# First attention of a two-layer sequence kernel: keys and receptances by seven block products

## The chip, the cores and the metric

The kernel runs on one core of one Trainium2 chip. The metric is the device time of one execution in microseconds (us). The core has engines that run side by side, each with its own queue in a fixed order: TensorE (PE in the profile; PEld are its weight loads) multiplies matrices into PSUM, VectorE (DVE) and ScalarE (ACT) work element by element and can read PSUM, GpSimd (POOL) works on SBUF alone, and SyncE (SP) issues most of the DMAs. An engine waits for another through semaphores, and an instruction that waits holds up all that stand behind it in its queue.

## The reference

Two layers, each an attention and a feed-forward part with a layer norm behind each. The change lies in the first attention, over 16 sequences of 256 tokens and 256 channels, with 16 heads of 128:

```python
xx = jnp.concatenate([jnp.zeros_like(hidden_states[:, :1]), hidden_states[:, :-1]], axis=1)
xk = hidden_states * time_mix_k + xx * (1.0 - time_mix_k)
xv = hidden_states * time_mix_v + xx * (1.0 - time_mix_v)
xr = hidden_states * time_mix_r + xx * (1.0 - time_mix_r)
receptance = jax.nn.sigmoid(jnp.einsum('bth,oh->bto', xr, Wr))
key = jnp.einsum('bth,oh->bto', xk, Wk)
value = jnp.einsum('bth,oh->bto', xv, Wv)
...
def step(state, inp):
    rt, kvt = inp                      # kvt = key * value
    out = (state + u * kvt) * rt       # u = time_first
    new_state = state * w + kvt        # w = exp(-exp(time_decay))
    return (new_state, out)
...
return jnp.einsum('bto,ho->bth', attn, Wo)
...
x = _layernorm(x + attention)
```

The first feed-forward part (gate, up and down products with dequantized integer weights) follows, then the second layer with another attention and a mixture of experts.

## The kernel before

The 4096 tokens are cut into 8 blocks of 512 (two sequences each). The first attention loops over blocks and, in each, over the 16 heads. Everything is float32, so that every matmul of the program appears as two instructions in the profile. The 256 input channels are two chunks of 128 rows, so each projection is two accumulating matmuls.

- `load_xT` (L296) brings the block's transposed input; `mixed` (L339) makes the three mixtures: a scaled copy `mt` on ScalarE (L346) and a multiply-add `xm` on VectorE (L349), two of each for a mixture. The next block's mixtures are traced in the middle of a block.
- `head` (L374) is one head: `project` (L360; matmul L363) for keys, receptances and values, each into a PSUM bank of 128x512 `proj`; ScalarE copies the keys to SBUF (`k_sb`, L380) and takes the sigmoid of the receptances (`r_sb`, L382); VectorE multiplies keys and values (`kv`, L384), scans along each of the two sequences (`st`, L389) and adds the first term (`su`, L398); GpSimd multiplies by the receptances (`wkv`, L407).
- `out_project` (L410; matmul L412) adds the head's output, four tiles of 128 tokens, into four PSUM tiles `o_ps` that gather all 16 heads. It runs two heads behind.
- `added` (L185) adds a finished block to `x` (L189) and normalizes it on VectorE (`moments`, L150 and L151; `rsqrt`, L141 and, on GpSimd, L142; `normalize`, L166).
- All weights of this stage are loaded at the start (L329, L333) and stay. `dequantized` (L255) turns the feed-forward's integer weights into float32 (L271 on VectorE); its loads are issued from ScalarE's queue, in block 0 behind head 12. The fills of two DRAM buffers (`res_d`, `xp_d`) are issued from SP, one DMA a block in blocks 1 to 5, each behind a sigmoid.

The order of the engines' queues in this stage is made by the framework's scheduler; `manual_schedule` blocks, in which the queues of the listed engines keep the order in which the program is traced, stand in later stages only.

## Time and profile before

| what | us |
|---|---|
| median of 4 runs | 2216.14 (2213.14 to 2216.55) |
| the profiled execution, its own time | 2211.11 |
| its span in the profile | 2209.3 |
| first matmul of the stage starts | 6.78 |
| last output matmuls of the stage (L412) start | 891.58 |
| first matmul of the feed-forward part (L208) starts | 894.61 |

A row of a group of instructions reads: line, engine, operation, output and inputs, shapes, count | busy time in us, mean ns of one | idle time of the engine just before them, and what ended most of it. A row of the timeline reads: start in us, duration in us (of the whole merged group), engine, line, operation, names, shapes, count, and in brackets the engine's idle time before it and what ended it. A row of the view of waits reads: who waited, for whom, us in total, times, longest. A matmul's duration in the rows contains its way through the array; the distance between the starts of two is what it costs in a full stream.

### The profile page before, as it was taken

To read this page: it belongs to the slowest core of one execution; us is meant where nothing else is said; L and a number is where in the kernel's file an instruction comes from. 1 tells how busy PE (TensorE), PEld (TensorE's weight loads), DVE (VectorE), ACT (ScalarE), POOL (GpSimd) and SP (SyncE) were. 2 spreads that over 40 slices of the span, in tenths; PEclk is the share of its full clock that TensorE was granted. 3 is DMA by queue.
4 is the path that set the end of the run, shared out by engine and by line. 5 is a ranking of instruction groups with operands and counts; after the bars stand their busy time and mean duration, and the time that the engine had idled before them with its cause. 6 is when DMAs were issued, how large, how long until landed. Compare 5 with 4: busy or idle time off the path is not lost. (4 is left out here: it accounts for less than half of the span.)

```text
span 2209.3 us, 26585 instructions
## 1 busy us (share of the span) xinstructions
PE 2106.3 (95%) x8776; PEld 1301.9 (59%) x8776; DVE 1258.2 (57%) x3468; ACT 779.6 (35%) x2205; POOL 831.3 (38%) x972
## 2 busy tenths in 40 slices
PE   8999999999999999999998999999999999979878
PEld 4555555555555555555564666666666666656656
DVE  4464535353535343232326669798887979863435
ACT  3121212121212111211314665656566565521323
POOL 3121212121212121000004555657576766733556
PEclk9999999999999999999998999999999999999989
DMA  9120202020300000300000000000000000041347
GB/s 288 45 97 1 86 1 86 0 86 0 102 1 0 0 1 1 89 15 19 1 0 1 1 1 1 23 8 6 3 4 2 3 3 2 10 180 51 102 144 275
DMA packets 78234, 96.13 MB, mean 44 GB/s; under 512 B 14495, under 2 KB 70023, under 8 KB 75920
## 3 DMA queue, kind: packets, MB, share of 16 engines
q1 hardware_dynamic: 62320, 81.95, 11.4%
q10 hardware_dynamic: 6560, 7.30, 1.0%
q0 software_dynamic: 9216, 5.19, 0.9%
q8 instruction: 69, 1.13, 0.2%
q14 instruction: 69, 0.57, 0.1%
HBM read 62.69 MB, written 49.61 MB: 51 GB/s over the span
## 5 line engine op out<-in xcount | busy, mean ns | idle before, releaser
L407 POOL TENSOR_TENSOR wkv<-su,r_sb 128x512 f32<-128x512 f32 x128 | 164.9, 1288 | 682.6 <-DVE su L398 646.8
L384 DVE TENSOR_TENSOR kv<-k_sb,proj 128x512 f32<-128x512 f32 x128 | 88.0, 687 | 412.7 <-PE proj L363 412.7
L971 POOL TENSOR_TENSOR pr<-pr,rr 128x256 f32<-128x256 f32 (+1 forms) x256 | 207.1, 836 | 158.7 <-DVE rr L969 111.7
L958 ACT ACTIVATE pr<-sm,nm 128x128 f32<-128x128 f32 (+1 forms) x512 | 226.5, 446 | 96.3 <-DVE nm L945 88.9
L380 ACT COPY k_sb<-proj 128x512 f32<-128x512 f32 x128 | 74.9, 585 | 522.3 <-PE proj L363 509.2
L363 PE MATMUL proj<-xm,w_Wk 128*128 128x512 f32 x512 | 242.5, 596 | 6.8 <-DVE xm L349 6.8
L412 PEld LDWEIGHTS o_ps<-w_o,wkv 128*128 128x128 f32 x1024 | 194.4, 190 | 90.9 <-issue 68.2
L412 PE MATMUL o_ps<-w_o,wkv 128*128 128x256 f32 x1024 | 245.2, 379 | 1.6 <-POOL xb L298 1.5
L363 PE MATMUL proj<-xm,w_Wv 128*128 128x512 f32 x512 | 240.7, 592 | 1.1 <-ACT r_sb L382 1.1
L363 PE MATMUL proj<-xm,w_Wr 128*128 128x512 f32 x512 | 240.8, 593 | 0.0
L934 PE MATMUL s_ps<-kT,qT 128*128 128x128 f32 (+1 forms) x1024 | 199.0, 338 | 25.1 <-DVE nm L945 20.8
L916 POOL TENSOR_TENSOR qT<-qT,turned 128x512 f32<-128x512 f32 x128 | 162.8, 1274 | 88.9 <-DVE turned L915 88.9
L934 PEld LDWEIGHTS s_ps<-kT,qT 128*128 128x128 f32 x1024 | 146.6, 194 | 46.4 <-issue 32.7
L988 ACT COPY aT<-a_ps 128x384 f32<-128x384 f32 x256 | 109.8, 481 | 171.9 <-PE a_ps L984 171.9
L363 PEld LDWEIGHTS proj<-xm,w_Wr 128*128 128x128 f32 x512 | 97.5, 190 | 119.6 <-issue 118.1
L363 PEld LDWEIGHTS proj<-xm,w_Wv 128*128 128x128 f32 x512 | 97.2, 190 | 117.6 <-issue 115.4
L389 DVE TENSOR_TENSOR_SCAN st<-decay,kv 128x255 f32<-128x255 f32 x256 | 164.2, 683 | 3.9
L945 DVE CUSTOM_DVE_ANT_0 sm<-s_ps,const 128x128 f32<-128x128 f32 (+1 forms) x512 | 154.1, 354 | 16.5 <-PE s_ps L934 13.5
L830 POOL DMA_INDIRECT xp_d<-xs,dest x128 | 132.2, 1033 | 57.1 <-issue 31.1
L363 PEld LDWEIGHTS proj<-xm,w_Wk 128*128 128x128 f32 x512 | 97.7, 191 | 77.3 <-issue 63.7
L142 POOL TENSOR_TENSOR rstd<-rs_t,nhalf 128x4 f32<-128x4 f32 (+1 forms) x33 | 33.1, 1004 | 273.4 <-DVE rs_t L141 272.7
L997 PE MATMUL c_ps<-aT,kf 128*64 128x256 f32 (+1 forms) x1024 | 111.5, 339 | 19.2 <-ACT aT L988 19.2
(176 smaller groups left out, 3278.4 us busy)
## 6 DMA issues: line engine op xcount, KB each, us to landing
res_d<-zeros SPq DMA_DIRECT2D x4, 4096.0 KB
res<-res_d SPq DMA_DIRECT2D x16, 1024.0 KB
w_e<-in_W_experts_dram SPq DMA_DIRECT2D x32, 384.0 KB
xp_d<-empty SPq DMA_DIRECT2D x1, 5440.0 KB
xe<-xp_d SPq DMA_DIRECT2D x32, 170.0 KB
xb<-in_xT_dram SPq DMA_DIRECT2D x16, 256.0 KB
xs<-in_x_dram SPq DMA_DIRECT2D x32, 128.0 KB
out_dram<-os ACTq DMA_DIRECT2D x7, 512.0 KB
```

What stands on the lines that cost most here:

```text
L363: nc.tensor.matmul(ps, lhsT=w3[name][:, c, h * P : (h + 1) * P], rhs=xm[:, c, :], start=(c == 0), stop=(c == DC - 1),)
L389: nc.vector.tensor_tensor_scan(st[:, s, 1:], decay[:, h : h + 1].to_broadcast([P, S - 1]), kv[:, s, : S - 1], 0.0, ALU.mult, ALU.add,)
L407: nc.gpsimd.tensor_tensor(wkv, su, r_sb, ALU.mult)
L412: nc.tensor.matmul(os[tt], lhsT=wkv[:, tt * P : (tt + 1) * P], rhs=w_o[:, h, :], start=(h == 0), stop=(h == NH - 1),)
L830: put = nc.gpsimd.indirect_dma_start(out=xp_d[:, :], out_offset=bass.IndirectOffsetOnAxis(ap=dest[:, k, t : t + 1], axis=0), in_=xs[b][:, ...
L916: nc.gpsimd.tensor_tensor(qT, qT, qr, ALU.add)
L934: nc.tensor.matmul(ps[:, lo:hi], lhsT=qT[:, s * S + i * P : s * S + (i + 1) * P], rhs=kT[:, s * S : s * S + hi - lo], start=True, stop=True,)
L945: nc.vector.tensor_tensor_reduce(out=sm[:, lo:hi], in0=self.ps[s][:, lo:hi], in1=cst["mask"][:, lo:hi], scale=-(DQ**-0.5), scalar=-MASKED, ...
L958: nc.scalar.activation(self.pr[:, s, lo:hi], self.sm[s][:, lo:hi], AF.Exp, bias=self.nm[:, s, i : i + 1], scale=-1.0, accum_out=self.rs[:, ...
L971: nc.gpsimd.tensor_tensor(self.pr[:, :, lo:hi], self.pr[:, :, lo:hi], rr[:, :, i : i + 1].to_broadcast([P, 2, hi - lo]), ALU.mult,)
L988: copy = nc.scalar.copy(aT, a_ps)
L997: mm = nc.tensor.matmul(c_ps[k * KVLR : (k + 1) * KVLR, s, i * P :], lhsT=kf[:, 2 * s + i, :KVLR], rhs=aT[:, : 2 * P] if i == 0 else aT[:, ...
```

## The change

Heads are taken in pairs. For one pair, the keys of two heads (2 x 128 outputs) over the block's two sequences (2 x 256 tokens) from two chunks of channels are a 2 x 2 by 2 x 2 block product, eight products of 128x128 weights with 256 columns of input. After the change they are seven products (the Winograd form of Strassen's method), of sums of weight blocks with sums of input blocks, each alone in half a PSUM bank, and the results are put together by additions on VectorE. The same goes for the receptances. The values keep their eight.

The parts:

- `seven` issues the seven matmuls into four PSUM tiles `one`, `two`, `five` and `end` (the pool's four banks), copies the first product to SBUF on ScalarE, and adds on VectorE: three additions of 128x512 and one of 128x256, each with one input in PSUM and each using the result of the one before.
- `weight_sums` makes the sums of weight blocks in block 0, by eight GpSimd operations of 128x128 a pair, and SP writes them to DRAM (`wsum_d`). From block 1 on `load_weights` reads them from there. Weights are no longer kept: three buffers each, loaded two pairs ahead by SP.
- `mixed` is a generator that makes one mixture at a time, with four subtractions of 128x256 for the keys' and the receptances': for block 0 on VectorE (keys) and GpSimd (receptances), for the later blocks on GpSimd. They are placed behind pairs 3, 4 and 5 of the block before.
- `Pair` holds the parts of `head`, the sigmoid now in place in SBUF. The stage runs inside `manual_schedule`: step m has the keys of pair m, then the second scan, `su`, wkv product and the output of the pair before, values, receptances and first scan of pair m.
- `out_project` gathers into two PSUM tiles of a whole bank. The first matmul into a bank in a block runs over 512 columns (the weights of head 0 and a block of zeros behind them) so that it clears the bank.
- `block_end` replaces `added`: the additions, the moments and the normalizing (now on ScalarE) are three pieces, placed in the following steps; those of the last block go into the feed-forward part, behind its first Silu.
- `dequantized` issues its loads from SP and is cut into ten pieces, one behind each pair of block 1 and the first two of block 2. Each fill becomes four DMAs, one behind every second pair.
- The states' zero columns and the exponentials of the decay are made once at the start.

The diff, cut to its core:

```diff
-        nc.scalar.dma_start(out=sc, in_=a[f"s_{name}"].partition_broadcast(P))
+        nc.sync.dma_start(out=sc, in_=a[f"s_{name}"].partition_broadcast(P))
...
-                nc.scalar.dma_start(out=q[at : at + n, :], in_=wq[c : c + n, :])
+                nc.sync.dma_start(out=q[at : at + n, :], in_=wq[c : c + n, :])
...
+            yield
+    A11, A12, S1, A22, S2, S3, S4 = range(7)
+    B11, B21, B22, T1, T2, T3, NT4 = range(7)
+    C11, C12, C21, C22 = range(4)
...
+        def weight_sums(w3, p, eng):
+            for i, n in enumerate(SUMS):
+                w = w3[n]
+                for to, x, y, op in (
+                    (S3, A11, S1, ALU.subtract),
+                    (S1, S1, A22, ALU.add),
+                    (S2, S1, A11, ALU.subtract),
+                    (S4, A12, S2, ALU.subtract),
+                ):
+                    eng.tensor_tensor(w[:, to, :], w[:, x, :], w[:, y, :], op)
                 nc.sync.dma_start(
...
+                    out=wsum_d[i * NPR + p], in_=w.rearrange("p k o -> p (k o)")
+                )
+
+        def mixed(xb, k_eng, r_eng):
+            for j, n in ((1, "Wv"), (0, "Wk"), (2, "Wr")):
+                xm = pm.tile([P, 4 if n == "Wv" else 7, S], F32, tag=f"xm{j}", name="xm")
...
+                if n != "Wv":
+                    eng = k_eng if n == "Wk" else r_eng
+                    for to, x, y in ((T3, B22, T1), (T1, T1, B11), (T2, B22, T1), (NT4, B21, T2)):
+                        eng.tensor_tensor(xm[:, to, :], xm[:, x, :], xm[:, y, :], ALU.subtract)
+                yield n, xm
+
+        def seven(w, x, dst):
+            one, two, five, end = [
+                ps_p.tile([P, 2, S], F32, tag="proj", name=f"{n}_ps") for n in ("p1", "p2", "p5", "p3")
+            ]
+            for to, at, bt in (
+                (one[:, 0], A11, B11),
+                (two[:, 0], A12, B21),
+                (two[:, 1], S2, T2),
+                (one[:, 1], S3, T3),
+                (five[:, 0], S1, T1),
+                (end[:, 0], S4, B22),
+                (end[:, 1], A22, NT4),
+            ):
+                nc.tensor.matmul(to, lhsT=w[:, at, :], rhs=x[:, bt, :], start=True, stop=True)
+            t = phd.tile([P, 1, S], F32, tag="t", name="t_sb")
+            nc.scalar.copy(t[:, 0], one[:, 0])
+            yield
+            add = nc.vector.tensor_tensor
+            add(dst[:, C11 : C12 + 1], t.to_broadcast([P, 2, S]), two, ALU.add)
+            add(dst[:, C21], dst[:, C12], one[:, 1], ALU.add)
+            add(dst[:, C12::2], dst[:, C12 : C21 + 1], five[:, 0:1].to_broadcast([P, 2, S]), ALU.add)
+            add(dst[:, C12 : C21 + 1], dst[:, C12 : C21 + 1], end, ALU.add)
+            yield
...
+        with tc.manual_schedule(engines=engines):
...
+            for m in range(NM + 1):
...
+                for e in ends:
+                    next(e)
+                if m == 0:
+                    new.values(0)
+                if new:
+                    keys = new.sums("Wk")
+                    next(keys)
+                if old:
+                    old.scan(1)
+                if new:
+                    if m == 0:
+                        xms.update(mixing)
+                    next(keys)
+                    if b == 0 and p + 1 < NPR:
+                        weight_sums(weights[0], p + 1, nc.gpsimd)
+                if old:
+                    old.add_first(1)
+                    old.times_r(1)
+                    old.out_project(0)
+                for e in ends:
+                    next(e)
+                if new:
+                    new.values(0 if m else 1)
+                    rec = new.sums("Wr")
+                    next(rec)
+                    new.scan(0)
+                    new.add_first(0)
+                    next(rec)
+                    sigmoid = new.sigmoid()
+                if old:
+                    old.out_project(1)
+                for e in ends:
+                    next(e)
+                ends = []
+                if old and old.p == NPR - 1:
+                    ends.append(block_end(old.b))
+                if new:
+                    if m:
+                        new.values(1)
+                    new.times_r(0)
+                    if p in (3, 4, 5) and b + 1 < NB:
+                        if p == 3:
+                            mixing, xms_next = mixed(xb, nc.gpsimd, nc.gpsimd), {}
+                        n, xm = next(mixing)
+                        xms_next[n] = xm
+                    if b in (1, 2):
+                        next(dequantizing, None)
+                    if p % 2 and 1 <= b <= K + 1:
+                        after(fill(b, p // 2), sigmoid, "in this block")
+                old = new
+        next(ends[0])
...
+                with tc.issue_after(last_of["ACT"]):
+                    for _ in ends[0]:
+                        pass
...
-        "Wr": v["L0_attn_Wr"].T,
-        "Wk": v["L0_attn_Wk"].T,
-        "Wv": v["L0_attn_Wv"].T,
+        "Wr": pairs(v["L0_attn_Wr"].T),
+        "Wk": pairs(v["L0_attn_Wk"].T),
+        "Wv": pairs(v["L0_attn_Wv"].T),
```

## The prediction

> **What bounds the kernel now.** I read the page's busy times first, then the stretch from 400 to 500 us, then the timeline of a few heads of the first attention. The page:
>
> ```profile
> PE 2106.3 (95%) x8776; PEld 1301.9 (59%) x8776; DVE 1258.2 (57%) x3468; ACT 779.6 (35%) x2205; POOL 831.3 (38%) x972
> ...
> L363 PE MATMUL proj<-xm,w_Wk 128*128 128x512 f32 x512 | 242.5, 596 | 6.8 <-DVE xm L349 6.8
> ```
>
> The stretch (PE, weight loads, DVE, ACT, POOL, clock, DMA share, GB/s) and the timeline, where a head's keys begin:
>
> ```profile
> 400.00:500.00 100.00, 100.00 (x291) 55.11 (x291) 49.10 (x82) 21.02 (x35) 21.03 (x32) 1.00 0.14 48
> ...
> 400.46 1.88 PE L363 MATMUL proj<-xm,w_Wk 128*128 128x512 f32 x4
> 405.61 1.89 PE L412 MATMUL o_ps<-w_o,wkv 128*128 128x256 f32 x8
> 405.88 0.69 DVE L384 TENSOR_TENSOR kv<-k_sb,proj 128x512 f32<-128x512 f32 x1 [4.03 <-PE proj L363]
> 406.61 1.27 DVE L389 TENSOR_TENSOR_SCAN st<-decay,kv 128x255 f32<-128x255 f32 x2
> 407.34 1.88 PE L363 MATMUL proj<-xm,w_Wk 128*128 128x512 f32 x4
> 407.98 0.75 DVE L398 SCALAR_TENSOR_TENSOR su<-kv,vecs,st 128x512 f32<-128x512 f32 x1
> ```
>
> TensorE never rests, at the full granted clock, and sets the end of this stage; VectorE is half busy. A head takes 407.34 - 400.46 = 6.88 us: 12 instructions of 512 columns at 0.43 (four keys in 402.18 - 400.46) and 8 of 256 at 0.215. So an instruction costs its columns, also at 256, where the loads (190 ns) just fit. A pair is 13.75 us, the stage 64 pairs.
>
> **The products.** Keys and receptances of a pair were 16 instructions of 512 columns (6.88 us); they become 2 x 7 products of 256 columns, two instructions each: 28 x 0.215 = 6.02. A pair falls to 12.89, and 64 x 0.86 = **-55.0 us**. Opening the paired output banks lets two matmuls of each block run over 512 columns instead of 256: 2 x 2 x 0.215 x 8 blocks = **+6.9**.
>
> **VectorE.** Each product set adds four VectorE additions, three of 512 columns and one of 256. The nearest rows have the same shapes, one input in PSUM and one in SBUF:
>
> ```profile
> L384 DVE TENSOR_TENSOR kv<-k_sb,proj 128x512 f32<-128x512 f32 x128 | 88.0, 687 | 412.7 <-PE proj L363 412.7
> L349 DVE SCALAR_TENSOR_TENSOR xm<-xb,rest,mt 128x512 f32<-128x512 f32 x48 | 38.9, 836 | 7.2 <-ACT mt L346 4.2 <-PE proj L363 2.6
> L189 DVE TENSOR_TENSOR xs<-o_ps,xs 128x256 f32<-128x256 f32 x32 | 13.0, 412 | 13.4 <-PE o_ps L412 13.4
> ```
>
> Each addition needs the one before it, so what counts is the step to a dependent instruction: 406.61 - 405.88 = 0.73, and 0.44 for 256 columns; four take 2.63. Bounds for a long one: 0.60 (an independent follower starts that soon in the trace, 130.82 to 131.42) and 0.84 (the xm row); I take 0.73, as kv is the same operation; at 0.60 the late steps below mostly vanish and the sum falls by 25, at 0.84 it rises by 44. Per pair VectorE has 2 x 2.63 of additions and 2 x (0.73 + 1.37 + 0.75) of kv, scans and su: 10.96, some 10.3 with independent ones overlapping, of 12.89.
>
> In a plain step, from its first key product: keys to 3.01, output of the older pair's first head to 4.73, values to 6.45, receptances to 9.46, output to 11.18, values to 12.89. VectorE: kv from 0.26 (0.26 after the values' last matmul, as at 405.88), scans to 2.6, key additions to 5.1, su to 5.8; kv at 6.7 when the values land, scans and su to 9.5, receptance additions to 12.1. Sigmoid and GpSimd's product follow to 14.3, 1.4 into the next step, where the output needs it at 3.0; the four product banks are free by 5.1 (wanted at 6.45) and 12.1 (wanted at 12.89). So a plain step stays with TensorE, and so does a block's end (four additions 1.7, statistics 2.4): **0**; without that spare 2 us each would cost its length.
>
> **Sharing between VectorE and GpSimd.** In the old order GpSimd's wkv falls into VectorE's rest. Where it did not:
>
> ```profile
> 223.21 1.27 POOL L407 TENSOR_TENSOR wkv<-su,r_sb 128x512 f32<-128x512 f32 x1 [5.57 <-DVE su L398]
> 223.59 2.10 DVE L349 SCALAR_TENSOR_TENSOR xm<-xb,rest,mt 128x512 f32<-128x512 f32 x2 [0.53 <-PE proj L363]
> ...
> 227.69 1.41 DVE L349 SCALAR_TENSOR_TENSOR xm<-xb,rest,mt 128x512 f32<-128x512 f32 x2
> ```
>
> The same pair takes 2.10 beside GpSimd and 1.41 without: it starts about 0.15 before GpSimd ends. kv, with an input in PSUM, is not held (0.68 at 125.98, beside a wkv), the scans are (1.62 for two at 126.69). So scans, su and mixing exclude GpSimd's products, one at a time.
>
> **Steps that mix the next block.** Three steps of blocks 0 to 6 end with two scaled copies on ScalarE and two VectorE mixes, traced behind the sigmoids; the second and third add four GpSimd subtractions. On VectorE: 2.0 idle after the last addition (0.15 to ScalarE, the two sigmoids 1.0, a copy 0.70, 0.15 back), mixes 1.36, kv and the wait for a subtraction 0.79, scans 1.27, additions 2.53, su 0.65, kv 0.73, a wait for the wkv product 0.61, scans 1.37, su 0.65, additions 2.63: 14.6, against 12.89. Queued behind the mixes is the kv that frees the keys' additions, and then TensorE waits for banks and for wkv. The first such step is absorbed by the spare 2 us; the next two lose 1.65 and 1.7, the recovery 1.2: 4.55 a block. Blocks 3 to 6: 18.2; block 2 with six small dequantizing pieces 5.3; block 1 with four of 1.03 us (0.82 and 0.21 at L271) 6.7: **+30.2**. A subtraction is 0.63 by the nearest row (128x256), bounds 0.63 and 1.04, the latter worth 13 in all:
>
> ```profile
> L971 POOL TENSOR_TENSOR pr<-pr,rr 128x512 f32<-128x512 f32 x128 | 133.5, 1043 | 0.0
> ...
> L971 POOL TENSOR_TENSOR pr<-pr,rr 128x256 f32<-128x256 f32 x128 | 80.4, 628 | 158.7 <-DVE rr L969 111.7 <-PE s_ps L934 16.5 <-DVE top L778 14.3
> ```
>
> **Weight sums.** In block 0 each step puts eight 128x128 operations on GpSimd ahead of the older pair's product. The line through the two rows gives 0.42 each (bounds 0.3 and 0.63), 3.4 a step: covered in plain steps. In the mixing steps subtractions (2.5), sums (3.4) and the waits between come before the product, which ends some 5 us late: **+6.5** for block 0, 5 to 13 at the bounds. From block 1 the sums come from DRAM: 18 blocks of 64 KB in 12.89 us, 92 GB/s of the 319 of the first 30 us, requested two steps (25.8 us) ahead on SP. Ahead of them there can stand a fill waiting for the sigmoid, up to 13 us, and four 1 MB fills a block. **0**; a load later than its two steps would stop TensorE for as long.
>
> **Start and end.** Before: first product at 6.78, then 2.1 lost until 19.18. After: values at 7.5, keys only when mixes and subtractions are done (10.3 to 14.8), receptances to 21.2, sigmoid with its 1.28 table load, wkv at 28; the third pair starts at 38.7 with 23.2 us of TensorE work done: 15.5 lost against 8.9, **+6.6**. At the end the last pair's scan, su and product follow one another: 3.05 idle against 0.35, **+2.7**. Half of the last block's normalizing goes behind the feed-forward's first Silu, on engines that are idle there: 0.
>
> **Dequantizing.** Its DMA issues leave ScalarE's queue for SP's, its pieces go to blocks 1 and 2 (costed above). Two losses of before vanish, 1.72 and 1.35 (keys 8.60 and 8.22 apart instead of 6.88 around 46 and 122): **-3.1**. One of the views of waits:
>
> ```profile
> PE o_ps L412 <- POOL xb L298: 1.5, 1, 1.5
> PE proj L363 <- ACT r_sb L382: 1.1, 1, 1.1
> ```
>
> The Trainium skill (Trainium Kernel Development and Optimization, Key Constraints) says that issuing DMAs from several engines only saves issue time, as all run on the same 16 engines. By that rule moving them gives nothing and the sum is 1.35 higher; the row shows ScalarE standing 6.4 and 6.7 us behind issues that wait, so I keep the gain.
>
> The skill's PSUM — Partial Sum Buffer (PSUM bank collisions raise a hardware error) forbids two engines in one bank at once. ScalarE's copy of the first product would then wait for the fourth, 1.29 later; no row of before shows half a bank being read. In the plain step it is done at 2.3 against scans ending at 2.6, so the sum is the same either way.
>
> **Sum.** -55.0 + 6.9 + 30.2 + 6.5 + 6.6 + 2.7 - 3.1 = **-5.2**. The profiled execution took 2211.11 (span 2209.3), so it would become 2205.9; the runs' median is 2216.14, so I forecast **2211 us**. A measurement here tells 0.2% (4.4 us) from no change.
>
> **Rivals.**
> 1. Sharing bites less: GpSimd's short operations slip between VectorE's. For: VectorE's short ones did (1353.79, 0.72 instead of 0.29, with GpSimd hardly delayed). Against: the 2.10 above. Mixing then costs 13.1 instead of 30.2, block 0 2.6 instead of 6.5, the start 1 less: **2189**. If ScalarE's part hides too, TensorE alone is left: 2211 - 30 - 6.5 - 4 = 2170.
> 2. Slower: VectorE's dependent chain is longer. If a long addition takes 0.78 and a short one 0.48, each loop grows by 0.38; over 20 late steps that is 7.6, block ends begin to stall (about 1 a block, 7 in all), and start, block 0 and end add 3: +18, **2229**. It decides above 0.76; at 0.84 it is 2255. For: three chained additions in place have no row; against: kv.
> 3. The change doesn't do what it says: 256-column products that wait on several engines don't run at 0.215. At 0.245 the 28 instructions take 6.86 and the gain of 55 is gone: about **2240** even if mixing then hides in part. Against: the eight output matmuls in 1.72 us.
>
> **How the numbers follow.** Forecast 0.42 (its own range 2203 to 2219: faster 0.24, same 0.12, slower 0.06), rival 1 0.30, rival 2 0.21 (same 0.03, slower 0.18), rival 3 0.07. Faster 0.54, same 0.15, slower 0.31. The range reaches to rivals 1 and 2 and so to the 0.60 of a long addition (2186) and the 0.78: 2186 to 2231.
>
> **What would show it.** Key products 12.9 us apart in plain steps; 14 to 15 behind the second and third mix, with TensorE waiting for wkv and for a key addition; VectorE above 80% busy in the stage; long additions near 0.69. Equal steps everywhere would speak for rival 1, plain steps over 13.2 for rival 2, 256-column products over 0.23 apart for rival 3. A TensorE wait for weights from DRAM would make the forecast wrong in a way that no case here has.

## The result and the profile after

The changed kernel takes **2218.66 us** (median of 37 runs, 2215.03 to 2221.12) against 2215.44 of the kernel before in the same runs (57 runs, 2209.72 to 2220.37). The ratio is 1.0015, with a 95% interval of 1.0011 to 1.002: 3.2 us slower by the medians, less than the 0.2% that was taken as the limit of what can be told from no change. The forecast was 2211 us, 5.2 faster. The profiled execution took 2215.1 us, its span is 2213.3 (before: 2211.11 and 2209.3).

The products became cheaper as foreseen, and almost the same amount was lost in other places of the same stage. The page's first part, and then the stretch from 400 to 500 us (columns as in the prediction), of the changed kernel:

```profile
PE 2081.5 (94%) x9544; PEld 1444.0 (65%) x9544; DVE 1613.2 (73%) x3960; ACT 759.7 (34%) x2237; POOL 919.4 (42%) x972
```

```profile
400.00:500.00 100.00, 96.71 (x379) 70.85 (x378) 89.29 (x138) 17.93 (x38) 28.23 (x30) 1.00 0.43 134
```

TensorE is busy for 24.8 us less in the whole program, but it now rests for 3.3 of these 100 us, where it did not rest at all. VectorE went from 49 to 89 busy of 100. The clock is still 1.00, and the weights' stream (DMA share 0.43, 134 GB/s) makes nothing wait: the view of TensorE's waits, cut to the first 920 us of the changed kernel, names VectorE and GpSimd only:

```profile
PE o_ps L512 <- POOL wkv L499: 22.5, 30, 3.8
PE p_ps L419 <- DVE Wk_sb L424: 7.9, 14, 0.8
PE v_ps L449 <- DVE xm L395: 6.8, 1, 6.8
```

The distance from one pair's first key product to the next one's, read from TensorE's timeline, tells where this happens. A plain step takes 12.93 us (13.755 before), and one that opens a block's output banks 13.785. A block without losses would take 7 x 12.93 + 13.785 = 104.3 us. Blocks 3, 4 and 6 take 110.0: their first mixing step 13.52, the second and third 15.20 each, the one behind them 13.53. These are the four steps that the prediction put at 12.89, 14.54, 14.59 and 14.09.

One of the late steps, from the timeline of the changed kernel over all engines (the step's keys start at 411.57):

```profile
412.75 1.15 ACT L494 ACTIVATE Wr_sb<-Wr_sb 128x512 f32<-128x512 f32 x2 [5.88 <-DVE Wr_sb L427]
...
413.81 1.32 ACT L388 ACTIVATE mt<-xb,mixes 128x512 f32<-128x512 f32 x2
414.55 1.42 DVE L395 SCALAR_TENSOR_TENSOR xm<-xb,rest,mt 128x512 f32<-128x512 f32 x2 [1.89 <-ACT mt L388]
...
415.88 0.68 DVE L463 TENSOR_TENSOR kv<-Wk_sb,v_ps 128x512 f32<-128x512 f32 x1
416.04 3.67 POOL L401 TENSOR_TENSOR xm<-xm 128x256 f32<-128x256 f32 x4 [1.31 <-DVE xm L395]
416.60 1.79 DVE L470 TENSOR_TENSOR_SCAN st<-decay,kv 128x255 f32<-128x255 f32 x2
...
419.01 3.44 PE L419 MATMUL p_ps<-xm,w_Wr 128*128 128x256 f32 x14 [0.52 <-DVE Wk_sb L424]
...
421.90 1.27 POOL L499 TENSOR_TENSOR wkv<-su,Wr_sb 128x512 f32<-128x512 f32 x1 [2.19 <-DVE su L483]
422.37 1.93 DVE L470 TENSOR_TENSOR_SCAN st<-decay,kv 128x255 f32<-128x255 f32 x2
423.22 1.99 PE L512 MATMUL o_ps<-w_o,wkv 128*128 128x256 f32 x8 [0.76 <-POOL wkv L499]
```

The reader is to see three things. VectorE stands still for 1.89 us until ScalarE's two sigmoids and a copy are done; everything of the next step is queued behind the two mixes. Two scans, 1.27 us alone, take 1.79 beside GpSimd's subtractions and 1.93 beside the wkv product. TensorE waits twice, 0.52 for the first key addition and 0.76 for wkv. VectorE itself has no other rest: from kv at 415.88 to the next step's kv at 431.08 it is one chain of 15.20 us, and that is the step.

A plain step of the same timeline, the one ahead of the first mix (its keys start at 385.12):

```profile
385.48 0.68 DVE L463 TENSOR_TENSOR kv<-Wk_sb,v_ps 128x512 f32<-128x512 f32 x1
...
386.20 2.30 DVE L470 TENSOR_TENSOR_SCAN st<-decay,kv 128x255 f32<-128x255 f32 x2
386.37 1.58 POOL L499 TENSOR_TENSOR wkv<-su,Wr_sb 128x512 f32<-128x512 f32 x1 [5.49 <-ACT Wr_sb L494]
...
391.10 0.74 DVE L483 SCALAR_TENSOR_TENSOR su<-kv,vecs,st 128x512 f32<-128x512 f32 x1
...
391.78 0.69 DVE L463 TENSOR_TENSOR kv<-Wk_sb,v_ps 128x512 f32<-128x512 f32 x1
392.01 1.27 POOL L499 TENSOR_TENSOR wkv<-su,Wr_sb 128x512 f32<-128x512 f32 x1 [4.07 <-DVE su L483]
392.50 1.90 DVE L470 TENSOR_TENSOR_SCAN st<-decay,kv 128x255 f32<-128x255 f32 x2
...
395.18 0.68 DVE L424 TENSOR_TENSOR Wr_sb<-t_sb,p_ps 128x512 f32<-128x512 f32 x1
395.96 0.42 DVE L425 TENSOR_TENSOR Wr_sb<-Wr_sb,p_ps 128x256 f32<-128x256 f32 x1
...
396.49 0.69 DVE L426 TENSOR_TENSOR Wr_sb<-Wr_sb,p_ps 128x512 f32<-128x512 f32 x1
397.28 0.69 DVE L427 TENSOR_TENSOR Wr_sb<-Wr_sb,p_ps 128x512 f32<-128x512 f32 x1
```

Both pairs of scans are held, by 2.30 - 1.27 = 1.03 and 1.90 - 1.27 = 0.63 us. The two products that hold them are those that VectorE has itself just released: su at 391.10 starts wkv at 392.01, and VectorE goes on at once with kv and the scans that run into it. The four receptance additions end at 397.97, 12.85 us into a step of 12.93. In this step the spare on which the prediction relied isn't there. Not every plain step is so tight: in the first one of the same block, from 345.47, VectorE waits 0.25 and 0.17 us for values, and run 2 below shows when the spare comes back. In the group table of the first 920 us this shows as a mean (the same row of before had 683 ns for a scan):

```profile
L470 DVE TENSOR_TENSOR_SCAN st<-decay,kv 128x255 f32<-128x255 f32 x256 | 232.1, 946 | 4.4
```

### The profile page after: what moved, and what is told of

Its sections match the earlier page's. It is cut to its first block, busy times and chain, and to the rows that moved or that the text cites. A ratio compares the mean times of both kernels' runs of the same rounds, so it can differ in the third digit from the quotient of the medians.

```text
span 2213.3 us, 29467 instructions
## 1 busy us (share of the span) xinstructions
PE 2081.5 (94%) x9544; PEld 1444.0 (65%) x9544; DVE 1613.2 (73%) x3960; ACT 759.7 (34%) x2237; POOL 919.4 (42%) x972
## 4 chain that ended last, share of the span: by engine, by line
PE 61%; DVE 26%; ACT 6%; issue 3%; POOL 1%; DMA 1%; another core or an unknown queue 1%; DVEq 0%; SPq 0%; POOLq 0%; ACTq 0%
PE p_ps L419 11%; PE o_ps L512 7%; PE v_ps L449 6%; PE g_ps L208 4%; PE u_ps L208 4%; DVE st L470 4%; PE s_ps L1102 4%; PE d_ps L247 3%; PE c_ps L1165 2%; DVE sm L1113 2%; PE o_ps L1184 2%; PE q_ps L1066 2%; PE a_ps L1152 2%; ACT pr L1126 2%; DVE turned L1083 2%
## 5 line engine op out<-in xcount | busy, mean ns | idle before, releaser
L499 POOL TENSOR_TENSOR wkv<-su,Wr_sb 128x512 f32<-128x512 f32 x128 | 168.8, 1318 | 576.1 <-ACT Wr_sb L494 333.0
L512 PE MATMUL o_ps<-w_o,wkv 128*128 128x256 f32 (+1 forms) x1024 | 253.5, 390 | 23.5 <-POOL wkv L499 22.5
L449 PE MATMUL v_ps<-xm,w_Wv 128*128 128x512 f32 x512 | 242.5, 596 | 6.8 <-DVE xm L395 6.8
L470 DVE TENSOR_TENSOR_SCAN st<-decay,kv 128x255 f32<-128x255 f32 x256 | 232.1, 946 | 4.4
L419 PE MATMUL p_ps<-xm,w_Wr 128*128 128x256 f32 x896 | 208.0, 382 | 8.6 <-DVE Wk_sb L424 7.9
L419 PEld LDWEIGHTS p_ps<-xm,w_Wr 128*128 128x128 f32 x896 | 167.7, 190 | 68.2 <-DVE Wk_sb L424 21.0
L419 PE MATMUL p_ps<-xm,w_Wk 128*128 128x256 f32 x896 | 204.3, 380 | 1.5 <-DVE Wr_sb L424 1.5
L419 PEld LDWEIGHTS p_ps<-xm,w_Wk 128*128 128x128 f32 x896 | 170.4, 190 | 52.8 <-issue 22.8
L494 ACT ACTIVATE Wr_sb<-Wr_sb 128x512 f32<-128x512 f32 x128 | 73.7, 623 | 309.7 <-DVE Wr_sb L427 276.8
L1113 DVE CUSTOM_DVE_ANT_0 sm<-s_ps,const 128x128 f32<-128x128 f32 (+1 forms) x512 | 154.2, 354 | 14.8 <-PE s_ps L1102 12.1
L449 PEld LDWEIGHTS v_ps<-xm,w_Wv 128*128 128x128 f32 x512 | 97.7, 191 | 75.1 <-issue 61.3
```

Source lines behind the costliest of these rows:

```text
L419: nc.tensor.matmul(to, lhsT=w[:, at, :], rhs=x[:, bt, :], start=True, stop=True)
L449: nc.tensor.matmul(ps, lhsT=self.w3["Wv"][:, 2 * h + c, :], rhs=self.xms["Wv"][:, 2 * c : 2 * c + 2, :].rearrange("p s t -> p (s t)"), sta ...
L470: nc.vector.tensor_tensor_scan(st[:, s, 1:], decay[:, n : n + 1].to_broadcast([P, S - 1]), kv[:, s, : S - 1], 0.0, ALU.mult, ALU.add,)
L499: nc.gpsimd.tensor_tensor(wkv, self.su[h], self.both(self.r, h), ALU.mult)
L512: nc.tensor.matmul(ps.rearrange("p t d -> p (t d)") if opens else ps[:, tt % 2, :], lhsT=self.wkv[h][:, tt * P : (tt + 1) * P], rhs=w_o[:, ...
L1113: nc.vector.tensor_tensor_reduce(out=sm[:, lo:hi], in0=self.ps[s][:, lo:hi], in1=cst["mask"][:, lo:hi], scale=-(DQ**-0.5), scalar=-MASKED, ...
```

## The experiments

Thirteen kernels ran, on four chips. The kernel before takes 2216.8 us on one of them and 2176.5 to 2177.8 on the three others, so each time stands beside that of the kernel before on its own chip, and ratios are to it. The stage itself runs alike on all four (a plain step of the seven products is 12.93 us in every trace), so the last column can be compared across them. All variants start from the changed kernel. For the first seven runs the theories were **V** (behind each mix the step is as long as VectorE's own chain, the idle time for ScalarE included), **G** (GpSimd's own queue, with subtractions and weight sums ahead of wkv, sets it) and **W** (the loss lies in the weights or in the plain steps).

| run | edit | us | before, same chip | ratio (95%) | first feed-forward matmul |
|---|---|---|---|---|---|
| changed kernel | | 2218.66 | 2215.44 | 1.0015 (1.0011 to 1.002) | 896.87 |
| 1 | copies ahead of sigmoids | 2149.51 | 2176.50 | 0.9873 (0.9856 to 0.9889) | 867.74 |
| 2 | no mixes in the loop | 2132.46 | 2176.50 | 0.9797 (0.978 to 0.9813) | 851.68 |
| 3 | subtractions on VectorE | 2197.67 | 2176.50 | 1.0096 (1.008 to 1.0113) | 916.78 |
| 4 | eight products again | 2183.63 | 2176.50 | 1.0032 (1.0023 to 1.0042) | 900.02 |
| 5 | run 1, weight sums behind wkv | 2187.35 | 2216.77 | 0.9866 (0.985 to 0.9882) | 863.76 |
| 6 | run 5, mixes spread out | 2190.43 | 2216.77 | 0.9882 (0.9866 to 0.9899) | 864.87 |
| 7 | subtractions behind wkv | 2223.28 | 2216.77 | 1.003 (1.0019 to 1.0041) | 898.17 |
| 8 | run 6, su in both places | 2176.53 | 2216.77 | 0.9814 (0.9797 to 0.9831) | 850.94 |
| 9 | su among key additions | 2161.72 | 2177.77 | 0.9929 (0.9916 to 0.9943) | 881.43 |
| 10 | su among receptance additions | 2166.12 | 2177.77 | 0.9946 (0.9932 to 0.996) | 883.75 |
| 11 | su in both places | 2151.29 | 2177.77 | 0.9881 (0.9866 to 0.9896) | 870.56 |
| 12 | run 5, su in both places | 2133.46 | 2177.77 | 0.9799 (0.9786 to 0.9812) | 851.19 |
| 13 | wkv cut to a quarter | 2155.10 | 2176.63 | 0.9897 (0.988 to 0.9913) | 872.24 |

### 1. ScalarE's copies ahead of the sigmoids

```diff
                     next(rec)
+                    if p in (3, 4, 5) and b + 1 < NB:
+                        ts = copies(xb, MIXTURES[p - 3][0])
                     new.scan(0)
                     new.add_first(0)
                     next(rec)
                     sigmoid = new.sigmoid()
...
-                        n, xm = next(mixing)
-                        xms_next[n] = xm
+                        xms_next[n] = mix_one(xb, j, n, ts, nc.gpsimd)
```

> The changed kernel with ScalarE's two scaled copies of a mixture traced before the receptances' additions and the sigmoids, the VectorE mixes left where they are. Theory V (behind each mix the step runs at VectorE's own chain, in which it idles 1.89 us for ScalarE's copy): the idle time before the mixes falls from 1.89 to nearly 0, steps of 15.2 us fall to 13.3 to 13.8, those of 13.5 to 12.93; 3 to 4 us a block in seven blocks, about 2192. Rival G (GpSimd's own load makes wkv late, as the releaser in the waits says): no change, within 3 us of 2219.

VectorE no longer waits ahead of a mix. Its timeline in this run, behind the receptance additions of a step that mixes:

```profile
401.31 1.41 DVE L401 SCALAR_TENSOR_TENSOR xm<-xb,rest,mt 128x512 f32<-128x512 f32 x2
...
403.35 2.12 DVE L506 TENSOR_TENSOR_SCAN st<-decay,kv 128x255 f32<-128x255 f32 x2
```

There is no bracket at 401.31, so no idle time. A block of 3 to 6 loses 0.8 to 1.1 us instead of 5.7. Had the waits of TensorE for wkv been a matter of GpSimd's queue (G), this edit would not have touched them; they fell from 22.5 to 11.1 us. The scans are still held (2.12).

### 2. No mixes from block 1 on

```diff
-                        if b:
-                            xms = xms_next
...
-                        n, xm = next(mixing)
-                        xms_next[n] = xm
```

> The changed kernel without the mixtures of blocks 1 to 7: all blocks use block 0's (left out: copies, mixes and subtractions of seven blocks). Theory V: every step from block 1 on but the opening ones at 12.93, dequantizing hidden; the surplus of blocks 1 to 6 (111.97, 110.94, 110.03, 110.02, 110.37, 110.02 against 104.3) goes, 38 us, and some 5 of block 0's: about 2176. Rival W (weights from DRAM or waits of plain steps cost as well): steps stay above 12.93 here and there, over 2185.

Every step behind the start is 12.93 us (13.785 with an opening, 13.03 to 13.10 in a few beside the dequantizing), and the stage ends 45.2 us sooner. So mixing costs all that blocks 1 to 6 and the late steps of block 0 lose, and W falls: a plain step is TensorE's alone, the weights' stream included.

This run also shows VectorE in plain steps that no mix disturbs. Its timeline, in the fourth step of a block (from 363.20) and the seventh (from 401.99):

```profile
363.40 0.69 DVE L463 TENSOR_TENSOR kv<-Wk_sb,v_ps 128x512 f32<-128x512 f32 x1
364.12 2.29 DVE L470 TENSOR_TENSOR_SCAN st<-decay,kv 128x255 f32<-128x255 f32 x2
...
402.19 0.69 DVE L463 TENSOR_TENSOR kv<-Wk_sb,v_ps 128x512 f32<-128x512 f32 x1 [0.91 <-PE v_ps L449]
408.66 0.69 DVE L463 TENSOR_TENSOR kv<-Wk_sb,v_ps 128x512 f32<-128x512 f32 x1 [0.82 <-PE v_ps L449]
...
413.52 0.69 DVE L427 TENSOR_TENSOR Wr_sb<-Wr_sb,p_ps 128x512 f32<-128x512 f32 x1
```

In the seventh step VectorE waits 0.91 and 0.82 us for values and ends its additions 12.2 us into the step. In the fourth it waits for nothing ahead of the first kv, its scans are held by 1.02 us, and the additions end at 12.69. Two steps earlier, around the opening, stands the work of the block's end (four additions and the moments). VectorE comes out of it late, and the wait ahead of the first kv returns only step by step: 0, 0.44, 0.70 and 0.91 us from the fourth step to the seventh.

### 3. Subtractions on VectorE

```diff
-                            mixing, xms_next = mixed(xb, nc.gpsimd, nc.gpsimd), {}
+                            mixing, xms_next = mixed(xb, nc.vector, nc.vector), {}
```

> The changed kernel with the subtractions of the later blocks' mixtures on VectorE instead of GpSimd. Theory V: VectorE's chain grows by 4 x 0.52 = 2.1 and loses a wait of 0.5 for GpSimd, in two steps a block: the steps of 15.2 become 16.5 or more, together some 15 to 20 us slower, about 2236. Rival G: GpSimd is relieved of 3.7 us in these steps, wkv comes earlier, faster than 2210.

With GpSimd relieved and VectorE's chain longer, the late steps of blocks 1 to 6 grow to between 15.9 and 17.2 us, and the wait for key additions, 7.9 in the changed kernel, is now TensorE's largest in its view of waits:

```profile
PE p_ps L419 <- DVE Wk_sb L424: 28.6, 15, 2.9
```

V holds, G does not.

### 4. Eight products in the order written by hand

The seven products, their sums and additions are left out; keys and receptances are computed as before, with ScalarE's copies.

```diff
-            for to, at, bt in (
-                (one[:, 0], A11, B11),
...
+            for h in range(2):
+                for c in range(DC):
+                    nc.tensor.matmul(
...
+            for h in range(2):
+                nc.scalar.copy(dst[:, 2 * h : 2 * h + 2, :], two[h])
```

> The changed kernel with eight products again for keys and receptances (accumulated in PSUM, two copies on ScalarE), no weight sums, no additions, no subtractions, weights streamed from their own DRAM tensors; the hand order kept. Theory V: steps of 12.93 + 0.86 = 13.79 everywhere, mixing hidden, no wait for wkv; blocks 111.2: 3 to 6 us slower than the changed kernel, 2222 to 2225, so that the seven products are worth no more than that. If the order itself cost time beside the products, it would be slower than 2230.

Behind the start the steps are 13.755 us everywhere, 14.61 with an opening, in mixing steps too. The whole is 0.3% slower than before, about what the opening alone costs (8 x 0.855 = 6.8 us), and the losses behind the mixes come with what the seven products bring along (additions, subtractions and weight sums, which this run doesn't tell apart), not with the order written by hand.

### 5. Weight sums of block 0 behind the wkv product

```diff
                     next(keys)
-                    if b == 0 and p + 1 < NPR:
-                        weight_sums(weights[0], p + 1, nc.gpsimd)
                 if old:
                     old.add_first(1)
                     old.times_r(1)
                     old.out_project(0)
+                if new and b == 0 and p + 1 < NPR:
+                    weight_sums(weights[0], p + 1, nc.gpsimd)
```

> The early copies of e1, and in block 0 the weight sums on GpSimd behind the older pair's wkv product instead of ahead of it. Theory V with the queue on GpSimd in block 0: the step of 18.35 us falls to 14 or less and the 3.5 us wait for wkv goes; 4 to 5 us faster than e1 (ratio to the kernel before 0.985). If GpSimd's queue is not what holds that step: no change against e1 (0.987).

In the changed kernel GpSimd's queue in block 0's worst step (18.28 us) reads, in the timeline over all engines:

```profile
84.59 2.39 POOL L376 TENSOR_TENSOR w_Wk<-w_Wk 128x128 f32<-128x128 f32 x4
86.93 3.00 POOL L376 TENSOR_TENSOR w_Wr<-w_Wr 128x128 f32<-128x128 f32 x4
...
89.90 1.26 POOL L499 TENSOR_TENSOR wkv<-su,Wr_sb 128x512 f32<-128x512 f32 x1
...
91.22 1.99 PE L512 MATMUL o_ps<-w_o,wkv 128*128 128x256 f32 x8 [3.84 <-POOL wkv L499]
```

and in this run:

```profile
82.96 1.27 POOL L535 TENSOR_TENSOR wkv<-su,Wr_sb 128x512 f32<-128x512 f32 x1 [1.39 <-DVE su L519]
84.19 3.10 POOL L376 TENSOR_TENSOR w_Wk<-w_Wk 128x128 f32<-128x128 f32 x4
```

The 5.39 us of sums stand behind the product instead of ahead of it, and the step is 12.93. The feed-forward's first matmul comes 4.0 us sooner than in run 1; in the whole program the two ratios (0.9866 and 0.9873) can't be told apart. This is the one place where GpSimd's own queue was the cause.

### 6. Mixes in two places, subtractions behind the next wkv

On top of run 5, half of each mix stands ahead of each kv, ScalarE's copies stand behind the keys' copy, and the subtractions behind the next step's wkv.

```diff
+                    if mixes_now:
+                        xm = xms_next[n] = mix_one(xb, j, n, ts, None, cs=(0,), subs=False)
                     new.scan(0)
...
+                        mix_one(xb, j, n, ts, None, xm, cs=(1,), subs=False)
+                        if n != "Wv":
+                            todo.append(xm)
```

> e5, with each mixture's two VectorE mixes in the two places where VectorE waits for the values in a plain step (one ahead of each kv), the copies behind the keys' copy, and the subtractions on GpSimd behind the next step's wkv. Theory V: all steps of blocks 2 to 6 at 12.93 but the opening one, block 1 near 106: some 6 us faster than e5, ratio 0.982; the floor without any mixing was 0.980 with block 0 included. If mixing costs by its length wherever it stands: no faster than e5.

Missed: it is 3.1 us slower than run 5, not faster (1.1 of it by the stage's end). The subtractions now run beside other scans; scans stay at a mean of 976 ns and the subtractions grow to 957. Spreading VectorE's work bought nothing while the scans were still held.

### 7. Only the subtractions behind the next wkv

```diff
                     old.times_r(1)
                     old.out_project(0)
+                    if todo:
+                        sub(todo.pop(), nc.gpsimd)
...
-                        n, xm = next(mixing)
-                        xms_next[n] = xm
+                        xm = xms_next[n] = mix_one(xb, j, n, copies(xb, j), None, subs=False)
+                        if n != "Wv":
+                            todo.append(xm)
```

> The changed kernel with one edit on GpSimd: the subtractions of a mixture stand behind the next step's wkv product instead of ahead of it. Theory V: in blocks 1 to 6 wkv waits for su, not for the subtractions, which are done by then; the scans held move from the first pair of scans to the second: within 5 us of the changed kernel, the gain there is in block 0. Rival G (wkv late because of GpSimd's queue): the 22.5 us of TensorE's waits for wkv go, ratio to the kernel before 0.992 or less.

Nothing gained (1.003): a block's mixing steps are 13.52, 14.67, 15.37 and 14.22, in sum 0.3 more than in the changed kernel, and TensorE's waits for wkv are 28.8 us instead of gone. G falls for blocks 1 to 6.

### 8. Run 6 with su between the first and second addition

```diff
             add(dst[:, C11 : C12 + 1], t.to_broadcast([P, 2, S]), two, ALU.add)
+            yield
             add(dst[:, C21], dst[:, C12], one[:, 1], ALU.add)
...
                     next(keys)
+                    if old:
+                        old.add_first(1)
+                    next(keys)
...
-                    new.add_first(0)
                     next(rec)
+                    new.add_first(0)
+                    next(rec)
```

> e6, with su between the first and the second addition of each product set, so that dependent additions no longer follow one another there and su is ready 2 us earlier. Theory V: e6 is at TensorE's pace nearly everywhere, so at most 2 us faster than e6 (0.981 to 0.982); later than e6 only if the product banks come free too late (above 0.984).

Missed by far: 13.9 us faster than run 6, and every step but one of 13.0 is down to TensorE's own length from block 0's third on. V as it stood did not foresee that a place in the order can be worth so much, so it was split for the last runs. **X**: VectorE's scans and GpSimd's wkv exclude each other, which lengthens the chain and takes the spare of the plain steps. **C**: only the gaps in the chain of dependent additions count.

### 9 to 11. The same move in one place and in both, on the changed kernel

The diff is that of run 8, with its keys' part alone, its receptances' part alone, and both.

> The changed kernel with one edit: su of the older pair's second head stands between the first and the second addition of the keys instead of behind all four, so GpSimd's wkv can start some 2 us sooner, beside additions that read PSUM, and is done when the next scans begin. Theory X (VectorE's scans and GpSimd's wkv exclude each other, and this is what lengthens the mixing steps beyond the chain): scans fall from 946 to about 800 ns, plain steps stay at 12.93, steps behind the second and third mix fall from 15.2 to about 14.2, the stage loses 15 to 25 us, ratio to before 0.990 to 0.995. Theory C (only the chain of additions counts, and su fills its 0.2 us gap): scans stay near 946, 0.2 us a mixing step, 4 us in all, ratio about 1.000.

> The changed kernel with one edit: su of the new pair's first head stands between the first and the second addition of the receptances instead of ahead of all four. Its wkv waits for the sigmoid anyway, so it starts no sooner. Theory X: scans stay near 946 ns and only the gap in the chain is filled, 0 to 4 us in all, ratio 1.000 to 1.0015. Theory C: as much as the same edit in the keys, about 4 us, ratio about 1.000.

> The changed kernel with su moved in both places. Theory X: what the edit in the keys gives and at most 4 us more, ratio 0.988 to 0.995, late steps about 14. Theory C: 8 us in all, ratio about 0.998.

Run 9, the timeline over all engines in a late step:

```profile
411.98 0.74 DVE L484 SCALAR_TENSOR_TENSOR su<-kv,vecs,st 128x512 f32<-128x512 f32 x1
...
413.15 0.69 DVE L427 TENSOR_TENSOR Wk_sb<-Wk_sb,p_ps 128x512 f32<-128x512 f32 x1
413.26 1.27 POOL L500 TENSOR_TENSOR wkv<-su,Wr_sb 128x512 f32<-128x512 f32 x1
413.95 0.69 DVE L428 TENSOR_TENSOR Wk_sb<-Wk_sb,p_ps 128x512 f32<-128x512 f32 x1
...
415.81 1.27 DVE L471 TENSOR_TENSOR_SCAN st<-decay,kv 128x255 f32<-128x255 f32 x2
```

GpSimd's product now runs beside additions with an input in PSUM, which keep their 0.69 us, and the scans behind it are back at 1.27. As X expected, the scans' mean is 792 ns, the plain steps are 12.93, and the late steps 13.92 and 14.53. A block of 3 to 6 loses 3.1 to 3.4 us.

Run 10, on the receptances, was missed by both theories: it gives 13.1 us back by the stage's end (X: 4 at most; C: about 4). VectorE's timeline in a plain step:

```profile
386.68 0.69 DVE L464 TENSOR_TENSOR kv<-Wk_sb,v_ps 128x512 f32<-128x512 f32 x1 [0.82 <-PE v_ps L450]
387.40 1.27 DVE L471 TENSOR_TENSOR_SCAN st<-decay,kv 128x255 f32<-128x255 f32 x2
388.87 0.69 DVE L424 TENSOR_TENSOR Wr_sb<-t_sb,p_ps 128x512 f32<-128x512 f32 x1 [0.20 <-ACT t_sb L421]
389.47 0.74 DVE L484 SCALAR_TENSOR_TENSOR su<-kv,vecs,st 128x512 f32<-128x512 f32 x1
390.13 0.41 DVE L426 TENSOR_TENSOR Wr_sb<-Wr_sb,p_ps 128x256 f32<-128x256 f32 x1
```

The direct gain is twice what I had counted: an independent instruction fills the gap behind the scans and that behind the first addition, and from the scans' end to the second addition a late step now takes 1.17 us (from 418.02 to 419.19) instead of 1.55 (424.30 to 425.85 in the changed kernel). The late steps fall by 0.4 to 0.6, to 14.62 and 14.78. The rest is the bracket at 386.68: VectorE has got ahead, stands waiting 0.82 us for the values, and by the time it comes to its scans the product that su released is over (1.27, not 1.90). So the hold depends on being late. Where VectorE is behind, it goes straight from su to kv to scans and into its own product; where it has spare, it waits for the values and misses it. Both moves together (run 11) nearly add up: 26.3 us by the stage's end, against 15.4 and 13.1 alone. X had allowed at most 4 on top of run 9; it is 10.9. A block of 3 to 6 loses 1.8 to 2.1. Block 0's worst step, where the weight sums stand ahead of wkv, grew in all three runs (21.30, 19.62 and 19.49 us instead of 18.28).

### 12. Copies early, weight sums behind, su in both places

> The version with ScalarE's copies ahead of the sigmoids and block 0's weight sums behind wkv (0.9866), with su moved in both places; the mixes stay together behind the sigmoids. Theory X: every step from block 1 on at 12.93 and the time of the best version so far, ratio 0.980 to 0.983. If the spreading of the mixes and subtractions was needed too, the late steps stay above 13.2 and the ratio above 0.984.

The mixes stay in one place behind the sigmoids, and all steps from block 2 on are at TensorE's 12.93 us, or 13.785 with an opening (block 1 has one of 13.36). The whole program takes **0.9799** of the time before, 44 us less, and beats both kernels; run 8 (0.9814, on another chip) can't be told from it. TensorE's waits for wkv in the stage, in the view of waits of this run, against 22.5 us in the changed kernel:

```profile
PE o_ps L549 <- POOL wkv L536: 2.5, 2, 1.4
```

### 13. GpSimd's product cut to a quarter

```diff
-                nc.gpsimd.tensor_tensor(wkv, self.su[h], self.both(self.r, h), ALU.mult)
+                nc.gpsimd.tensor_tensor(wkv[:, :P], self.su[h][:, :P], self.both(self.r, h)[:, :P], ALU.mult)
...
-                        lhsT=self.wkv[h][:, tt * P : (tt + 1) * P],
+                        lhsT=self.wkv[h][:, :P],
```

> The changed kernel with GpSimd's product cut to 128 of its 512 columns (three quarters of the attention's weighted sum are left out; the output matmuls read those 128 columns four times, so TensorE has the same work). No order and no VectorE instruction is changed: it takes away most of the time in which GpSimd holds VectorE. Theory X (the scans that stand behind su run into the product that su has just released, in every step, so VectorE needs 12.5 of a plain step's 12.93 us and has no spare to absorb a mix): scans fall from 946 to 700 to 760 ns, VectorE's busy time in a plain step from 12.05 to about 10.5, the first mixing step goes back to 12.93, the later two to 14 to 14.6, a block of 3 to 6 loses 2.5 to 3.5 us instead of 5.7, ratio to before 0.988 to 0.993. Rival (the chain of dependent additions alone has used up VectorE's spare): scans fall, but the first mixing step stays at 13.5 and the later two at about 15, ratio 0.998 or more.

This run left the order and VectorE's instructions alone. VectorE's timeline, a plain step and the first mix behind it:

```profile
375.36 0.69 DVE L463 TENSOR_TENSOR kv<-Wk_sb,v_ps 128x512 f32<-128x512 f32 x1 [0.84 <-PE v_ps L449]
376.08 1.27 DVE L470 TENSOR_TENSOR_SCAN st<-decay,kv 128x255 f32<-128x255 f32 x2
...
381.82 0.69 DVE L463 TENSOR_TENSOR kv<-Wk_sb,v_ps 128x512 f32<-128x512 f32 x1 [0.82 <-PE v_ps L449]
382.54 1.27 DVE L470 TENSOR_TENSOR_SCAN st<-decay,kv 128x255 f32<-128x255 f32 x2
...
389.26 1.42 DVE L395 SCALAR_TENSOR_TENSOR xm<-xb,rest,mt 128x512 f32<-128x512 f32 x2 [1.89 <-ACT mt L388]
```

The scans' mean is 715 ns. VectorE's busy time in this plain step is 10.20 us of 12.93 (12.05 in the changed kernel), and it waits for values twice. The first mixing step is back at 12.93, though VectorE stands 1.89 us for ScalarE as before; the later two are 13.67 and 14.53, and a block of 3, 4 or 6 loses 2.3 us instead of 5.7, a little less than X's 2.5. The rival's 13.5 and 15 did not come. So with the product short, 3.4 of a block's 5.7 us go and 2.3 stay. These are not parts that add up: run 1 took away only VectorE's wait for ScalarE, left the scans held, and 4.6 to 5.0 of the 5.7 went, since no step can fall below TensorE's 12.93 and either takes off much of the same surplus. wkv also lands 0.8 us sooner here, which the run can't take apart from the hold. But a late step is VectorE's unbroken chain, which an earlier wkv does not shorten: from kv to the next step's kv it takes 14.54 us here (404.60 to 419.14), and 15.20 less the hold of 0.66 at 422.37 is 14.54 too.

## Why the prediction was wrong

Its terms beside what the trace of the changed kernel shows:

| term | predicted | measured |
|---|---|---|
| products, 64 pairs | -55.0 | 64 x (12.93 - 13.755) = -52.8 |
| opening of banks | +6.9 | 8 x (13.785 - 12.93) = +6.8 |
| mixing steps, blocks 1 to 6 | +30.2 | 7.67 + 6.65 + 5.73 + 5.72 + 6.08 + 5.72 = +37.6 |
| block 0 (13.89, 18.28 and 14.87 against 12.93) | +6.5 | +8.2 |
| start (third pair at 36.74 with 23.28 of work done; 8.9 lost before) | +6.6 | +4.6 |
| end of the stage | +2.7 | +0.7 |
| two losses of before, gone | -3.1 | -3.1 |
| sum | -5.2 | +2.0 |

The trace agrees with the measured sum: the feed-forward's first matmul starts at 896.87 instead of 894.61, 2.3 us later. The span grew by 4.0; the remaining 1.7 lie behind this stage, are less than what executions of one kernel differ by (2215.03 to 2221.12), and no run looks into them.

**The step that failed** is the size of the mixing term, where the prediction says: "The first such step is absorbed by the spare 2 us; the next two lose 1.65 and 1.7, the recovery 1.2: 4.55 a block." Measured in blocks 3, 4 and 6 it is 0.59, 2.27, 2.27 and 0.60, in all 5.73. Over the stage the term was put at +30.2 and is +37.6, and these 7.4 us alone outweigh the 5.2 that the sum promised. The products (2.2 short, as a plain step is 12.93 and not 12.89) and block 0 (1.7) add to the miss; the start and the end, overpriced by 4.0 together, hide part of it by luck. The mechanism, its places and the waits it named were right: VectorE's 2.0 us for ScalarE (1.89), TensorE's waits for wkv and a key addition, VectorE above 80%. Two sizes were not.

- **The spare.** The plain step was laid out from a clean start, with receptance additions done at 12.1, a block's end was put at 0, and GpSimd's exclusion was charged in the mixing steps only. The layout is right for a settled step (12.2 in the seventh step of run 2), and a block's end costs TensorE nothing in its own steps. But it leaves VectorE late, and a late VectorE meets the wkv products and recovers slowly. In the two plain steps between the opening and the first mix the receptance additions end at 13.38 and 12.85, and in the second of them the scans are held by 1.03 and 0.63 us. So the mix finds no spare to absorb it. Run 13, with the product short, has it back in that same step: VectorE waits 0.84 and 0.82 us for values, and its busy time is 10.20 us, near the 10.3 of the prediction, instead of 12.05.
- **The late step.** VectorE's loop was put at 14.6 and is 15.20. Of the difference of 0.61, scans beside the subtractions make +0.43 (1.70 instead of 1.27 from scan to addition), the two sets of additions +0.16 each (2.69 and 2.79 instead of 2.53 and 2.63); ScalarE's part, shorter by 0.11, and small ones take 0.14 off again.

The other points:

- **Chained additions** follow at 0.78 to 0.79 us, and 0.53 behind the short one (395.18, 395.96, 396.49, 397.28), where kv gave 0.73 and 0.44. That is rival 2's 0.78 and beyond its deciding point of 0.76. Its mechanism came true; it priced it at 18 us, and with everything else the result stands 8.4 above the forecast's own -5.2 (3.2 + 5.2). The block ends that it expected to stall did not (13.785 with an opening).
- **Rival 1** (sharing bites less, mixing 13.1) did not happen, but run 13 is nearly its case, and its blocks 1 to 6 lose 15.9 in sum.
- **Rival 3** falls: fourteen instructions of 256 columns take 3.02 us (385.12 to 388.14), 0.216 each.
- **Block 0**: right in kind, short by 1.7. A weight sum takes 624 or 570 ns there, not 420, and a subtraction 859, not 630: GpSimd is held by VectorE too.
- **Start and end** were overpriced by 2.0 each. At the end TensorE waits 0.38 and 1.42 us, against 0.60 before. Eight of the feed-forward's transposes fill part of the wait, and four that stood ahead of its first matmul (0.4 us) now stand behind it; the working counted on neither.
- **The two losses of before** are gone, but the prediction books them under the DMA issues that leave ScalarE's queue. In the trace of before TensorE's first wait (46.58, for GpSimd) comes ahead of these issues, and its second (122.28, for a sigmoid) 6.9 us behind the last of them. No run shows what moving the issues was worth alone.
- **The rule on sharing.** The Trainium skill (SBUF — State Buffer, Who interferes with whom) says that VectorE and GpSimd share a pair of ports under an exclusive lock, that an instruction of VectorE with two SBUF inputs contends there with one of GpSimd that reads SBUF, one with at most one SBUF input does not outside its two-port modes, and that the order of issue decides who waits. The changed kernel and runs 9 and 13 agree: scans 1.90 to 2.30 us beside a wkv, 1.27 without one; additions with one input in PSUM 0.69 either way.
- **The rule on banks.** The prediction weighed the skill's PSUM — Partial Sum Buffer (PSUM bank collisions raise a hardware error). ScalarE's copy of the first product does start only 1.98 us after the set's first instruction (391.58 to 393.56), behind the fourth product of 0.43 each. In the changed kernel VectorE comes later than that; in run 10 an addition waits 0.20 for it. The trace shows this order, not what would happen without it.
- **No cost** was right for the weights' stream: no wait of TensorE's in the stage names a load from DRAM.

## What to carry to other kernels

When an engine that had rest becomes nearly full, count its work in the plain steps with all that can hold it, those behind a disturbance above all, and not only in the step that looks hard: whether it has 2 us of spare or none decides what every later disturbance costs. Where one engine releases another's work and then contends with it, look at what it does next; giving it something that doesn't contend (here additions from PSUM between su and the next scan) was worth more than moving work to another engine or spreading it. Fill the gap behind a dependent instruction with an independent one, and put a copy that an engine must wait for ahead of longer work in its producer's queue.

## What the runs showed of the hardware

- The hold between VectorE and GpSimd feeds on itself: the same four scans took from 683 ns each (before) to 981 (run 5) with no scan changed, and saving 0.38 us in a late step gave back 13.1 us in the stage (run 10), where 0.38 in each of the 14 late steps would be 5.3.
- It works both ways: a GpSimd subtraction of 128x256 takes 0.73 us in block 0's start and 0.92 on average in the late step shown (four in 3.67), and four weight sums of 128x128 take 2.39 to 3.10.
- Three in-place additions that follow one another are 0.10 us further apart than their busy time (0.79 against 0.69); an instruction that doesn't depend on the one before starts 0.60 after it. An independent one between two of them costs less than its own length: with su (0.74) between them the first two additions of run 10 are 1.26 apart, 0.48 more than the 0.78 without it.
